# Cross-attention on one core: x in slices and Wo through ScalarE's queue, later weight loads, earlier residuals

## The chip, the cores and the metric

The kernel runs on one core of one Trainium2 chip, in float32. The metric is device microseconds of one execution. "us" is left out where a number is plainly a time.

The engines are named as the profile names them: PE (TensorE, matmuls; PEld is its weight load), DVE (VectorE), ACT (ScalarE), POOL (GpSimd) and SP (SyncE, which here only issues DMAs). A "q" behind an engine's name (ACTq, SPq) stands for that engine's instruction queue, where DMAs are issued and semaphores are waited for.

## The reference

x is (2, 2048, 640); the context is (2, 154, 1024), of which the first 77 rows are text and the other 77 an image prompt. There are 20 heads of 32.

```python
q = split_heads(x @ Wq.T)
k, v = split_heads(text @ Wk.T), split_heads(text @ Wv.T)
k_ip, v_ip = split_heads(ip @ Wk_ip.T), split_heads(ip @ Wv_ip.T)
out_text = softmax(q @ k.T / sqrt(32)) @ v
out_ip = softmax(q @ k_ip.T / sqrt(32)) @ v_ip
result = merge_heads(out_text + out_ip) @ Wo.T + bo + x
```

## The kernel before

**Tiles and steps.** Everything is kept transposed, with channels on partitions. The 4096 tokens (both batches) are cut into NBLK = 4 blocks of 1024 tokens, and the 640 channels into NC = 5 chunks of 128, which are four heads each. One step m = 5 j + c handles chunk c of block j; there are 20 steps, and one more round to finish the last. Blocks 0 and 1 are batch 0, blocks 2 and 3 batch 1.

**What one step does.** Scores of step m (L210) are computed in three groups of token tiles (3, 3 and 2) into the eight PSUM banks, LOW and HIGH four each. ScalarE copies them out (L222), VectorE takes maxima (L229), GpSimd subtracts them (L230), ScalarE takes the exponential (L236), VectorE sums (L243) and inverts (L245), GpSimd multiplies (L250), VectorE transposes 32 by 32 blocks (L261). In the same step TensorE also attends for step m - 1 (L273), whose result ScalarE copies to aT (L285), and it fills its time with other matmuls: `queries` for coming steps (L181, copied to qT by L189), and in steps 0 to 4 the keys and values of the next chunks (`project_kv`, L139, copied by L146 and L149), in later steps the output projection of finished blocks (`Out.step`, L308). An output piece of 128 channels by 512 tokens is finished on VectorE (`Out.store`, L319) with the bias and a residual piece of x that `Out.fetch` loads (L303), and is stored (L322).

**What sets the order.** The schedule is written out by hand: each engine runs its instructions in the order in which the code issues them, within the main loop over m. `plan(m)` names the filler work of a step in two lists, `after1` (behind the first two groups of scores) and `after2` (behind attention). `ahead` is how many of `after1` come before the first group's exponential (`soften(m, 0)`); the rest comes after it.

**DMAs before the change.** All but five loads of Wq at the start are issued from SyncE. They are, in the order of the code:

- `load_w` (L130): one 128-column piece of Wk, Wk_ip, Wv or Wv_ip, 512 KB, into one of five slots in the second aT buffer. It is called after every `project_kv`, which has freed a slot.
- `spread_v(c, b)` (L161): 16 small DMAs of 20 KB that copy the transposed V of chunk c (`vS`, written by `square_v`, L152) to four partition groups. Batch 0's are issued in steps 0 to 4, batch 1's in steps 6 to 10.
- `load_x` (L168): the next block of x as two loads of 1,280 KB, in the steps with c = 1.
- Wo (L495): one load of 1,600 KB at the end of step 4, into the space that held the context.
- the residuals, fetched up to FETCH = 3 pieces ahead of the stores, beginning in step 5, and the stores.

Of the kernel before, what the change touches and what calls it, by code (L numbers as in the profile page):

```python
# [19 lines left out]
def kernel(  # L20
# [25 lines left out]
    nc = tc.nc  # L46
    P = 128
    NC = C // P
    NCC = CC // P
    G = P // D  # L50
    TB = 512
    NH = 2
    BLK = NH * TB
    NT = BLK // P
    NBLK = B * S // BLK
# [6 lines left out]
    NM = NBLK * NC  # L62
# [4 lines left out]
    FETCH = 3  # L67
# [12 lines left out]
    def turn_to(half, n=G):  # L80


        turn[:] = half[:1] if n == 1 else (half[: min(n, G) - 1] + half[-1:]) * 2

    def bank():
        return turn.pop(0)
# [5 lines left out]
    xs = [const.tile([P, NC, BLK], F32, name=f"x_{n}") for n in range(2)]  # L92
# [14 lines left out]
    wo = wo_ct.rearrange("p (k o) -> p k o", k=NC)  # L107
# [6 lines left out]
    def block_of(m):  # L114

        j, c = divmod(m, NC)
        return j, c, j * BLK // S
# [7 lines left out]
    def load_w():  # L125
        n = len(loaded)
        if n < len(wlist):
            src, c = wlist[n]
            w = wslots[n % len(wslots)]
            nc.sync.dma_start(  # L130
                out=w, in_=src[:, ts(c, P)].rearrange("(k p) o -> p k o", p=P)
            )
            loaded.append(w)

    def project_kv(n, t):

        out = bank()[:, : B * L].rearrange("p (b l) -> p b l", b=B)
        for k in range(NCC):
            nc.tensor.matmul(  # L139
                out, loaded[n][:, k, :], cT[:, k, :, t, :], start=(k == 0), stop=(k == NCC - 1)  # L140
            )
        load_w()
        return out

    def project_k(c, t):
        nc.scalar.copy(kT[:, c, :, t, :], project_kv(4 * c + t, t))  # L146

    def project_v(c, t):
        nc.scalar.copy(vTs[c % 2][:, :, ds(t * L, L)], project_kv(4 * c + 2 + t, t))  # L149
# [7 lines left out]
    def spread_v(c, b):  # L157

        for g in range(G):
            for r in range(G):  # L160
                nc.sync.dma_start(  # L161
                    out=v4[r * D : (r + 1) * D, c, g].rearrange("p k d -> p (k d)"),
                    in_=vS[g * D : (g + 1) * D, c, b],
                )


    def load_x(j, h):
        nc.sync.dma_start(  # L168
            out=xs[j % 2][:, :, ts(h, TB)],
            in_=xT[:, ds(j * BLK + h * TB, TB)].rearrange("(c p) s -> p c s", p=P),  # L170
        )

    qTs = {}

# [28 lines left out]
    def scores(m, s, ps):  # L203

        _, c, b = block_of(m)
        first, n = GROUPS[s]
        for t in range(n):
            h, st = divmod(first + t, TB // P)
            for g in range(G):
                nc.tensor.matmul(  # L210
                    ps[g][:, ts(t, 2 * L)],
                    qTs[(m, h)][g * D : (g + 1) * D, ts(st, P)],
                    kT[g * D : (g + 1) * D, c, b].rearrange("p t l -> p (t l)"),
                    start=True,
                    stop=True,
                )

    def take(m, s, ps):

        n = GROUPS[s][1]  # L220
        for g in range(G):
            nc.scalar.copy(  # L222
                keys_of(m, s)[:, :, g], ps[g][:, : n * 2 * L].rearrange("p (n l) -> p n l", n=n)
            )
# [9 lines left out]
    def exponential(m, s):  # L234
        e = keys_of(m, s).rearrange("p n g l -> p (n g) l")
        nc.scalar.activation(e, e, AF.Exp, scale=SCALE)  # L236
# [3 lines left out]
    def sums(m, s):  # L240
        n = GROUPS[s][1] * G
        den = small.tile([P, n, 2], F32, tag=f"den{n}", name=f"den_{m}_{s}")
        nc.vector.tensor_reduce(den, rows_of(m, s), AX.X, ALU.add)  # L243
        rden = small.tile([P, n, 2], F32, tag=f"rden{n}", name=f"rden_{m}_{s}")
        nc.vector.reciprocal(rden, den)  # L245
        rdens[s] = rden

    def normalise(m, s):
        n = GROUPS[s][1] * G
        nc.gpsimd.tensor_tensor(  # L250
            rows_of(m, s), rows_of(m, s), rdens[s].unsqueeze(3).to_broadcast([P, n, 2, L]), ALU.mult
        )

    def soften(m, s):
        exponential(m, s)
        sums(m, s)
        normalise(m, s)

    def transpose(m, s):
        first, n = GROUPS[s]  # L260
        nc.vector.transpose(  # L261
            tT[:, first : first + n].rearrange("p n g k s -> p (n g k s)"),
            pb_of(m, s).rearrange("p n g l -> p (n g l)"),
        )
# [59 lines left out]
    outs = [Out(v) for v in range(NV)]  # L324
# [23 lines left out]
    def flush():  # L348
        for o in finished[len(stored) :]:
            o.store()  # L350
            stored.append(o)
            for o in outs[len(stored) : len(stored) + FETCH]:
                o.fetch()
# [15 lines left out]
    for k in (0, half):  # L369
        nc.sync.dma_start(  # L370
            out=wo_ct[:, ds(k * B * LT, half * B * LT)].rearrange("p (k n) -> p k n", k=half),
            in_=ctxT[ds(k * P, half * P), :].rearrange("(k p) n -> p k n", p=P),
# [17 lines left out]
    for t in range(2):  # L390
        project_k(0, t)

    def plan(m):

        q = [lambda h=h: queries(m + LEAD[h], h) for h in range(NH)]
        out = lambda: fill(NC)
        if m < NC:
            v = [lambda t=t: project_v(m, t) for t in range(2)]
            k = [lambda t=t: project_k(m + 1, t) for t in range(2) if m + 1 < NC]
            return q[:1] + v, k + q[1:]  # L400
        if m == NM - 1:
            return [out], [out] + [lambda: fill(NC - 1)] * OPEN
        if m == NM - 2:
            return [out], [out, q[1]]
        if m % NC == 0:
            return q, [out] * 2
        return [out, q[0]], [out, q[1]]

    def is_late(m):


        return m == NC or (m > NC and m % NC == 1)

    for m in range(NM + 1):
        j, c, _ = block_of(m)
        new = m < NM
        old = m >= 1
        after1, after2 = plan(m) if new else ([], [])
        flush()
        if new:  # L420
            for g, half in ((0, LOW), (1, HIGH)):
                scores(m, g, half)
            for g, half in ((0, LOW), (1, HIGH)):
                take(m, g, half)
        turn_to(LOW, len(after1))


        ahead = len(after1)
        if ahead > 1 and 2 < m < NM - 2 and c > 0:
            ahead -= 1  # L430
        short = new and (len(after1) == 1 or m == 0)
        late = is_late(m)
        if old and not late:
            transpose(m - 1, 2)
        if new:
            maxima(m, 0)
        if late:
            transpose(m - 1, 1)
        if new and not short:
            maxima(m, 1)  # L440
        if late:
            transpose(m - 1, 2)
        if c == 1 and j + 1 < NBLK:
            for h in range(NH):
                load_x(j + 1, h)
        for work in after1[:ahead]:
            work()
        flush()
        if new:
            if short:  # L450
                maxima(m, 1)
            else:
                soften(m, 0)
        for work in after1[ahead:]:
            work()
        flush()
        if m < NC:
            square_v(m)
            spread_v(m, 0)
        if new:  # L460
            scores(m, 2, HIGH)
        if old:
            attend(m - 1, LOW)
        if new:
            take(m, 2, HIGH)
            maxima(m, 2)
            if short:
                soften(m, 0)
                if old:
                    take_attention(m - 1, LOW)  # L470
            soften(m, 1)
            if short:
                soften(m, 2)
        if old:
            if not short:
                take_attention(m - 1, LOW)
            attended[(m - 1) // NC] += 1
            if (m - 1) // NC == NBLK // B - 1:
                spread_v((m - 1) % NC, 1)
        turn_to(HIGH, len(after2))  # L480
        if new:
            transpose(m, 0)
        for work in after2[:-1]:
            work()
        flush()
        if new and not short:
            soften(m, 2)
        for work in after2[-1:]:
            work()
        if m >= NC and (c == 0 or m == NM - 2):  # L490
            flush()
        if new and not is_late(m + 1):
            transpose(m, 1)
        if m == NC - 1:
            nc.sync.dma_start(out=wo, in_=WoT.rearrange("(c p) o -> p c o", p=P))  # L495
    turn_to(LOW)
    while len(finished) < NV:
        fill(NC)
# [33 lines left out]
```

## Time and profile before

Three executions took 538.38, 538.55 and 1334.83; the median is 538.55.

| | us |
|---|---|
| profiled execution | 538.22 |
| its span, first to last instruction | 536.4 |
| ScalarE waiting for queries (L189 <- PE L181), total | 99.5 |
| SyncE waiting to store (L322 <- DVE L319), total | 247.8 |
| one residual, 256 KB, issue to landing, median | 3.3 |
| one `load_x`, 1,280 KB, issue to landing, median | 8.7 |
| one spread, 20 KB, issue to landing, median | 1.8 |
| Wo, 1,600 KB, issue to landing | 7.0 |

The mean granted TensorE clock is 0.993. The DMA traffic is uneven: the page's 40 slices go from 9 to 308 GB/s, with a mean of 94. A time such as 61.75 below is counted from the start of the span. Step 1 begins with its scores at 45.08, step 2 at 74.48, step 3 at 97.73, step 4 at 121.55 and step 5 at 140.59. A matmul record counts passes: one score matmul of L210 makes two records, so "x24" are the 12 matmuls of one group of three tiles.

### The profile page before, as it was taken

The numbers are of one execution on the slowest core, as the hardware profiler recorded it, in microseconds if no ns is written. First come the engines' busy times: TensorE is split into PE (matmuls) and PEld (weight loads), VectorE is DVE, ScalarE is ACT, GpSimd is POOL, SyncE is SP. The second block draws the span as 40 slices with busy tenths as digits, with TensorE's granted clock in tenths as the row PEclk, the third lists the DMA queues.
The fourth block names the chain that finished last, engine by engine and source line by source line (L and its number), as shares of the span: only waits on it lengthen the run. The fifth ranks groups of instructions, "written<-read, shape, count | busy, mean of one in ns | idle before, by whom it ended". The sixth has DMA issues, their size and how long they took to land.

```text
span 536.4 us, 12754 instructions
## 1 busy us (share of the span) xinstructions
PE 522.8 (97%) x5614; PEld 289.0 (54%) x5614; DVE 378.1 (70%) x286; ACT 245.1 (46%) x441; POOL 351.0 (65%) x130
## 2 busy tenths in 40 slices
PE   8999799999999999999999999999999999999997
PEld 4676668677554545545454554544455454554442
DVE  0059765877878879787768978787678878888121
ACT  1255445456654444644454464445356464562000
POOL 0057947796967868668677866869576876978000
PEclk9999799999999999999999999999999999999999
DMA  8974733320136420221206311111112111131151
GB/s 258 308 208 138 243 94 88 97 59 9 32 138 221 150 89 25 82 65 48 57 16 221 144 41 40 42 39 42 38 41 75 45 42 40 40 101 40 61 187 67
DMA packets 50488, 50.60 MB, mean 94 GB/s; under 512 B 5248, under 2 KB 34432, under 8 KB 50432
## 3 DMA queue, kind: packets, MB, share of 16 engines
q1 hardware_dynamic: 49712, 49.45, 30.3%
q8 instruction: 44, 0.72, 0.6%
q10 hardware_dynamic: 720, 0.33, 0.2%
q14 instruction: 12, 0.10, 0.1%
HBM read 36.00 MB, written 10.49 MB: 87 GB/s over the span
## 4 chain that ended last, share of the span: by engine, by line
PE 87%; DVE 4%; issue 2%; DMA 2%; POOL 2%; ACT 1%; SPq 0%; ACTq 0%; DVEq 0%; POOLq 0%
PE bank L181 30%; PE bank L308 30%; PE bank L273 11%; PE bank L210 8%; PE bank L139 8%; DVE den L243 2%; POOL pb L250 2%; DVE mx L229 1%; DMA x<-in_x_dram 1%; ACT pb L236 1%; DVE ot L319 1%; DMA wq<-in_L_xattn_Wq_dram 1%; DMA res<-in_x_dram 1%; POOL pb L230 0%; DVE tT L261 0%
## 5 line engine op out<-in xcount | busy, mean ns | idle before, releaser
L230 POOL TENSOR_TENSOR pb<-pb,mx 128x1848 f32<-128x1848 f32 (+1 forms) x60 | 175.8, 2942 | 105.9 <-DVE mx L229 105.9
L250 POOL TENSOR_TENSOR pb<-pb,rden 128x1848 f32<-128x1848 f32 (+1 forms) x60 | 176.0, 2942 | 36.9 <-DVE rden L245 27.7
L181 PE MATMUL bank<-x,wq 128*128 128x512 f32 x400 | 180.0, 599 | 0.9 <-DMA x<-in_x_dram 0.9
L308 PE MATMUL bank<-aT,wo_ct 128*128 128x512 f32 x400 | 179.1, 599 | 0.9 <-ACT aT L285 0.9
L243 DVE TENSOR_REDUCE den<-pb 128x24 f32<-128x1848 f32 (+1 forms) x60 | 111.3, 1856 | 62.3 <-ACT pb L236 62.2
L229 DVE TENSOR_REDUCE mx<-pb 128x24 f32<-128x1848 f32 (+1 forms) x60 | 109.6, 1848 | 43.3 <-ACT pb L222 42.3
L236 ACT ACTIVATE pb<-pb 128x1848 f32<-128x1848 f32 (+1 forms) x60 | 95.1, 1587 | 87.4 <-POOL pb L230 87.4
L181 PEld LDWEIGHTS bank<-x,wq 128*128 128x128 f32 x400 | 75.4, 191 | 92.8 <-issue 87.4
L308 PEld LDWEIGHTS bank<-aT,wo_ct 128*128 128x128 f32 x400 | 73.7, 190 | 91.8 <-issue 83.8
L261 DVE STREAM_TRANSPOSE tT<-pb 128x1920 f32<-128x1920 f32 (+1 forms) x60 | 115.9, 1931 | 5.3 <-POOL pb L250 5.2
L222 ACT COPY pb<-bank 128x462 f32<-128x462 f32 (+1 forms) x240 | 101.1, 533 | 22.5 <-PE bank L210 21.2
L273 PE MATMUL bank<-tT,v 32*32 32x256 f32 x3200 | 70.5, 386 | 4.1 <-issue 3.6
L189 ACT COPY qT<-bank 128x512 f32<-128x512 f32 x40 | 23.4, 585 | 99.5 <-PE bank L181 99.5
L210 PEld LDWEIGHTS bank<-kT,qT 32*128 32x128 f32 x1280 | 44.7, 184 | 30.2 <-issue 19.6
L273 PEld LDWEIGHTS bank<-tT,v 32*32 32x32 f32 x3200 | 46.9, 103 | 21.9 <-issue 8.7
L210 PE MATMUL bank<-kT,qT 32*128 32x154 f32 x1280 | 54.8, 303 | 2.5 <-DVE ot L319 1.9
L319 DVE SCALAR_TENSOR_TENSOR ot<-bank,bo_sb,res 128x512 f32<-128x512 f32 x40 | 29.5, 739 | 37.6 <-PE bank L308 31.9
L139 PEld LDWEIGHTS bank<-wo_ct,aT 128*128 128x128 f32 x320 | 45.5, 197 | 5.2 <-issue 3.3
L139 PE MATMUL bank<-wo_ct,aT 128*128 128x154 f32 x320 | 46.9, 305 | 0.5 <-ACT pb L222 0.5
L285 ACT COPY aT<-bank 128x256 f32<-128x256 f32 x80 | 24.4, 391 | 17.2 <-PE bank L273 17.2
L245 DVE RECIPROCAL rden<-den 128x24 f32<-128x24 f32 (+1 forms) x60 | 17.2, 286 | 2.1
L146 ACT COPY kT<-bank 128x154 f32<-128x154 f32 x10 | 2.8, 286 | 15.1 <-PE bank L139 15.1
(12 smaller groups left out, 14.0 us busy)
## 6 DMA issues: line engine op xcount, KB each, us to landing
res<-in_x_dram SPq DMA_DIRECT2D x40, 256.0 KB, 3.3
out_dram<-ot SPq DMA_DIRECT2D x40, 256.0 KB, 2.4
x<-in_x_dram SPq DMA_DIRECT2D x6, 1280.0 KB, 8.7
v<-vS SPq DMA_DIRECT2D x160, 20.0 KB, 1.8
x<-in_x_dram SPq DMA_DIRECT2D x10, 256.0 KB, 5.0
aT<-in_L_xattn_Wk_dram SPq DMA_DIRECT2D x5, 512.0 KB, 7.0
aT<-in_L_xattn_Wk_ip_dram SPq DMA_DIRECT2D x5, 512.0 KB, 4.4
aT<-in_L_xattn_Wv_dram SPq DMA_DIRECT2D x5, 512.0 KB, 5.5
```

The costliest lines, as they stand in the source:

```text
L139: nc.tensor.matmul(out, loaded[n][:, k, :], cT[:, k, :, t, :], start=(k == 0), stop=(k == NCC - 1))
L181: nc.tensor.matmul(pq, wq[:, k, ts(c, P)], xs[j % 2][:, k, ts(h, TB)], start=(k == 0), stop=(k == NC - 1),)
L210: nc.tensor.matmul(ps[g][:, ts(t, 2 * L)], qTs[(m, h)][g * D : (g + 1) * D, ts(st, P)], kT[g * D : (g + 1) * D, c, b].rearrange("p t l -> ...
L222: nc.scalar.copy(keys_of(m, s)[:, :, g], ps[g][:, : n * 2 * L].rearrange("p (n l) -> p n l", n=n))
L229: nc.vector.tensor_reduce(mx, rows_of(m, s), AX.X, ALU.max)
L230: nc.gpsimd.tensor_tensor(rows_of(m, s), rows_of(m, s), mx.unsqueeze(3).to_broadcast([P, n, 2, L]), ALU.subtract)
L236: nc.scalar.activation(e, e, AF.Exp, scale=SCALE)
L243: nc.vector.tensor_reduce(den, rows_of(m, s), AX.X, ALU.add)
L250: nc.gpsimd.tensor_tensor(rows_of(m, s), rows_of(m, s), rdens[s].unsqueeze(3).to_broadcast([P, n, 2, L]), ALU.mult)
L261: nc.vector.transpose(tT[:, first : first + n].rearrange("p n g k s -> p (n g k s)"), pb_of(m, s).rearrange("p n g l -> p (n g l)"),)
L273: nc.tensor.matmul(pa[r][g * D : (g + 1) * D, : NT * D], v4[rows, c, g, k, :], tT[rows, :, g, k, :], start=(k == 0), stop=(k == NK - 1),)
L308: nc.tensor.matmul(self.po, wo[:, self.k, ts(self.o, P)], aTs[self.j % 2][:, self.k, ts(self.h, TB)], start=(self.k == 0), stop=(self.k == ...
```

## The change

- x of the next block is cut into ten slices of 256 KB (one chunk of channels, 512 tokens). They are put on a list in step 1 and then in the steps with c = 0 from step 5 on, and up to four of them are issued in a step, from ScalarE's queue, behind the last exponential of the step.
- Wo is issued from ScalarE's queue, in step 4, right behind the copies of the attention result. The first three residuals are asked for there too, on SyncE.
- `load_w` is called after a projection of K as before, but for V it is called inside `spread_v`, after the first four and after the first eight of the 16 small DMAs.
- The condition `c > 0` on `ahead` goes, so that in the steps 5, 10 and 15 the second of the two query projections is issued behind the first exponential.

No engine's arithmetic changes; the order of instructions on PE, DVE and POOL stays as it was. On ScalarE 31 DMAs come in between and one copy changes its place in three steps; on SyncE the DMAs are moved as said.

```diff
@@ project_kv / project_k
-        load_w()
         return out
     def project_k(c, t):
         nc.scalar.copy(kT[:, c, :, t, :], project_kv(4 * c + t, t))
+        load_w()
@@ spread_v
                     in_=vS[g * D : (g + 1) * D, c, b],
                 )
+            if b == 0 and g < 2:
+                load_w()
-    def load_x(j, h):
-        nc.sync.dma_start(
-            out=xs[j % 2][:, :, ts(h, TB)],
-            in_=xT[:, ds(j * BLK + h * TB, TB)].rearrange("(c p) s -> p c s", p=P),
-        )
+    slices = []
+    def load_x():
+        if slices:
+            j, h, k = slices.pop(0)
+            nc.scalar.dma_start(
+                out=xs[j % 2][:, k, ts(h, TB)], in_=xT[ts(k, P), ds(j * BLK + h * TB, TB)]
+            )
@@ main loop, before the work of after1
         ahead = len(after1)
-        if ahead > 1 and 2 < m < NM - 2 and c > 0:
+        if ahead > 1 and 2 < m < NM - 2:
             ahead -= 1
...
-        if c == 1 and j + 1 < NBLK:
-            for h in range(NH):
-                load_x(j + 1, h)
+        if m == 1 or (m >= NC and c == 0 and j + 1 < NBLK):
+            slices.extend((j + 1, h, k) for h in range(NH) for k in range(NC))
@@ main loop, behind the attention of m - 1
             if not short:
                 take_attention(m - 1, LOW)
             attended[(m - 1) // NC] += 1
+            if m == NC - 1:
+                nc.scalar.dma_start(out=wo, in_=WoT.rearrange("(c p) o -> p c o", p=P))
+                for o in outs[:FETCH]:
+                    o.fetch()
@@ main loop, end of a step
         if new and not short:
             soften(m, 2)
+        for _ in range(4):
+            load_x()
         for work in after2[-1:]:
             work()
...
-        if m == NC - 1:
-            nc.sync.dma_start(out=wo, in_=WoT.rearrange("(c p) o -> p c o", p=P))
```

## The prediction

> **What bounds the kernel now.** Times are in us. I read the page's busy shares first, then who waited for whom.
>
> ```profile
> PE 522.8 (97%) x5614; PEld 289.0 (54%) x5614; DVE 378.1 (70%) x286; ACT 245.1 (46%) x441; POOL 351.0 (65%) x130
> ...
> PEclk9999799999999999999999999999999999999999
> ```
>
> TensorE is the bound: it idles only 536.4 - 522.8 = 13.6 of the span, so hardly more than that can be won, while any wait put before it adds in full. Only the fifth of the 40 slices (53.6 to 67) has a lower clock. The list of waits (engine and line, what it waited for, total, times, longest) says where the idle time is; the second answer is of SyncE's queue:
>
> ```profile
> PE bank L273 <- issue: 3.6, 3, 2.7
> ...
> PE bank L210 <- DVE ot L319: 1.9, 2, 1.3
> ```
>
> ```profile
> SPq L366 <- DMA wq<-in_L_xattn_Wq_dram: 2.0, 1, 2.0
> ```
>
> The first two are this change's targets. The third is SyncE's queue at the start: a load of x held back for a load of Wq on another engine's queue, with which it shares no data. The built program says why: all DMAs use eight completion semaphores in turn, and each waits, at its issuer, for the DMA that had the same one before. I come back to that. Next the 1-us windows round the first stall (busy PE, PEld, DVE, ACT, POOL; then granted clock, DMA share, GB/s):
>
> ```profile
> 61.00:62.00 1.00, 0.00 (x0) 0.00 (x0) 0.97 (x4) 1.00 (x1) 0.50 (x1) 0.81 1.22 301
> 62.00:63.00 1.00, 0.77 (x19) 0.24 (x19) 1.00 (x2) 0.41 (x2) 1.00 (x1) 0.50 0.54 130
> ...
> 68.00:69.00 1.00, 1.00 (x8) 1.00 (x7) 0.00 (x0) 0.08 (x1) 1.00 (x1) 0.78 0.12 28
> ```
>
> TensorE stands from 59.5 to 62.2 waiting for no engine, and starts as the DMA traffic drains: I read it as its own instructions stuck behind x (two 1,280 KB loads issued at 48.05) and the weights of 53.56 and 55.67. The clock then stays at 0.50 until 68. The chain of waits prices that: the 32 matmuls of L139 take 6.91 there and 4.41 at 89.09 (2.5), the last 19 of L273 1.12 against about 0.4 (160 take 3.39): 3.2 lost to the clock. This stall costs 2.7 + 3.2 = 5.9.
>
> **Part 1: x away from SyncE, weights later (m = 1).** With 2,560 KB of x and 1,024 KB of weights gone from 48 to 59, I count the 5.9 as won. What is late next? In program order ScalarE's queue gets four x slices at the end of m = 1, after the last exponential and before the copy of qT. By the built program they wait for the landing of the 11th to 14th of the 16 spreads of V; SyncE issues those one by one:
>
> ```profile
> 61.75 10.55 SPq L161 DMA_DIRECT2D v<-vS  x16
> ...
> 74.59 0.58 ACT L189 COPY qT<-bank 128x512 f32<-128x512 f32 x1 [2.87 <-PE bank L181]
> ```
>
> One spread takes 10.55 / 16 = 0.66. They start after VectorE's transpose of V at 61.27, which hangs on the softmax chain and not on the stall, so still at 61.75. Two weight loads now lie among the first eight (0.6 each with the gap). The 14th starts at 61.75 + 13 x 0.66 + 1.2 = 71.5, lands 1.8 later (the spreads' median; 73.3), the slice takes 0.45 to issue (Wq slices on ScalarE: median 453 ns), the copy 0.58: 74.4. That ScalarE's engine stands while its queue issues is seen at the start: five issues from 0.73 take 2.34, its table load begins at 3.10. TensorE without the stall runs 59.65 (end of attention) + 4.4 (keys) + 4.3 (queries) + 0.9 (the first 24 score matmuls) = 69.3, then needs the bank that this copy empties: it stands 5.1. That is longer than the 2.7 which cost the clock before, so the clock falls again: +3.2. Net -5.9 + 5.1 + 3.2 = +2.4. Bounds: -0.8 if the clock holds; +3.9 if a spread lands 3.3 after its issue (the slowest at m = 2), being queued behind 512 KB of weights.
>
> **m = 2**, the same with no stall to win back:
>
> ```profile
> 89.85 10.77 SPq L161 DMA_DIRECT2D v<-vS  x16
> ...
> 97.73 1.85 PE L210 MATMUL bank<-kT,qT 32*128 32x154 f32 x48
> 97.83 0.58 ACT L189 COPY qT<-bank 128x512 f32<-128x512 f32 x1 [1.47 <-PE bank L181]
> ```
>
> 14th spread at 89.85 + 13 x 0.67 + 1.2 = 99.8, landed 101.6, slice issued 102.1, copy done 102.6; TensorE needs it at 97.73 + 0.9 = 98.7. Stall 4.0 to 5.5 by the same landing bounds; I take 4.3, since most land at 1.8. With the clock 7.5 (4.0 to 8.7). At m = 3 two slices wait for the 9th and 10th spread: 112.05 + 9 x 0.68 + 0.6 + 1.8 = 120.6, before the copy at 121.66: nothing.
>
> **Part 2: Wo on ScalarE's queue (m = 4).** It is queued right after the attention copies and waits for the 12th spread; behind it are the last exponential and the qT copy:
>
> ```profile
> 134.82 10.82 SPq L161 DMA_DIRECT2D v<-vS  x16
> ...
> 141.23 0.56 ACT L189 COPY qT<-bank 128x512 f32<-128x512 f32 x1
> ...
> 141.85 1.07 PE L210 MATMUL bank<-kT,qT 32*128 32x154 f32 x24 [0.20 <-ACT qT L189]
> ```
>
> ScalarE reaches it at 137.0 (copies of L285: 135.80 + 1.20). The 12th spread starts at 134.82 + 11 x 0.68 = 142.3, lands 144.1; issue 0.53 (as on SyncE), exponential 1.24 (now at 140.09), copy 0.57: 146.4 in place of 141.8. TensorE waits for exactly this copy already (0.20), so all of 4.6 shows, and with the clock 7.8 (4.6 to 9.3). SyncE saves that one issue, which nobody waited for.
>
> **Part 3: residuals early; one more query behind the softmax.** The second store of m = 5 waits 1.2 for its residual and TensorE 1.3 for that store (166.27, 167.08). Asked for at m = 4, the residual has landed: -1.3; VectorE is next at 165.1, when TensorE has just come. Without "c > 0" the exponentials at m = 5, 10, 15 go ahead of a query copy, which at m = 10 frees them from 271.0 back to about 268.4; the stores come earlier, and the other 0.6 of the wait on L319 goes. Nobody waits for the copy put behind. Together -1.9 (0 to -2.5).
>
> **Part 4: the other slices.** Issuing 4 x 0.45 = 1.8 per step lies in ScalarE's idle time before the copy of qT (3.92 to 4.91 at m = 6 and 7); uncovered it would cost up to 1.8. The fourth slice of m = 6 and of m = 10 waits for the first's landing, 3.4 (residuals of equal size) to 5.0 (x at the start): at m = 6 ScalarE is free at 188.8 to 190.4, wanted at 189.8; at m = 10 at 283 to 287, wanted at 284.4. I take +0.6 in all (0 to 4). SyncE's later DMAs wait for slices in turn; the residuals lie three outputs ahead: nothing.
>
> **Sum.** 2.4 + 7.5 + 7.8 - 1.9 + 0.6 = +16.4. The profiled execution took 538.22 (span 536.4), 0.3 under the median of the runs: 538.55 + 16.4 = 555.
>
> **Two rules beside these rows.** The Trainium skill ("TensorE: Matmul & The Clock Gate", Part 1) has the clock fall after an idle window of about 3.4 us and return after a busy one; here 2.7 sufficed, and the half clock lasted 6 after work resumed. By the page each fall would cost some 1.7, an estimate, and the sum be near 550. "DMA: Bandwidth & Descriptors" (Issuing engines are not separate DMA queues) says that DMAs from SyncE and ScalarE share the same 16 engines and that a second issuer saves only issue time; by it the move itself is worth nothing, which speaks against this change; the 5.9 would come from timing alone.
>
> **The rivals.** (a) *The clock does not fall* in the three new stalls: 555 - 3 x 3.2 = 545. For it: the wait of 1.3 at 167 left it at 1.00. Against: 2.7 did not, and these are 4 to 5. (b) *The stalls do not come* and the kernel is faster: ScalarE passes its DMAs because the spreads have landed, or runs on past them. Price: -5.9 - 1.9 = -7.8, 531. It decides if the 14th spread of m = 2 lands by 98, that is if the spreads take 0.4 and not 0.67 each. For it: ScalarE is busy only 46%. Against: SyncE's spread rows are alike at m = 1, 2 and 4. (c) *The change does not do what it says*: the fetch stall stays, as weights alone hold it up. Then the wait of m = 1 lies under it: 555 - 2.4 = 553.
>
> **Chances.** Forecast 0.62 (its own range 548 to 563), (a) 0.15, (b) 0.15, (c) 0.06, anything else 0.02. From 541 to 563 holds the forecast, (a) and (c) with their bounds, and leaves out (b). Beyond 2% (10.8, about what a measurement can tell from no change): slower than 549.3 are the forecast and (c), 0.65; (a), (b) and the forecast's lower end are within, 0.32; below 527.8 lies only what goes beyond (b), 0.03.
>
> **What would show it.** Fetch step: no "issue" wait of 2.7 for L273 near 59.5, clock 1.00 from 60 to 68. Stalls: ScalarE's queue waiting on DMA v at the lines of x and Wo, 4 to 7 at m = 1, 2, 4; TensorE's L210 waiting some 4 to 5 each for the qT copy; three dips to 0.50. Residuals: no wait of L319 for a DMA at 166. Wrong if ScalarE's DMA lines show no wait.

## The result, and the profile after

The changed kernel takes 555.0, the median of six runs (552.9 to 556.68), against 537.85 before, the median of six runs in all (536.99 to 538.55, and the one of 1334.83). The ratio is 1.0316, with a 95% interval from 1.0286 to 1.0345: slower, and the predicted time is met. The one execution of 1334.83 lies far above all others and is not in the ratio. The profiled execution took 555.08; its span is 553.3, which is 16.9 more than before, at a mean granted clock of 0.981.

The page's busy shares and its row of the clock, after the change:

```profile
PE 527.3 (95%) x5614; PEld 290.1 (52%) x5614; DVE 378.9 (68%) x286; ACT 245.8 (44%) x441; POOL 351.0 (63%) x130
...
PEclk9999979799979999999999999999999999999999
```

TensorE runs the same 5614 matmul records, so no work was added, but it idles 553.3 - 527.3 = 26.0 in place of 13.6, and is busy 4.5 longer for the same records. One dip of the clock (slice 5, counted from 1) has become three (slices 6, 8 and 12). The list of TensorE's waits:

```profile
PE bank L216 <- ACT qT L195: 15.2, 3, 5.4
PE bank L279 <- issue: 2.5, 3, 1.3
...
PE bank L187 <- DMA x<-in_x_dram: 0.8, 1, 0.8
```

The first line is new: the score matmuls (L210 before, L216 now) stand three times for the copy of qT on ScalarE. The attention's wait without a releaser has its longest at 1.3, no longer at 2.7, and the wait on the output store (L210 on L319 before, now L216 on L325) is gone from the list. The last line is no news: it lies at 9.8 to 10.6, where the kernel starts, and such a wait of 0.9 was there before. What held ScalarE up is in the same list for ScalarE:

```profile
ACT qT L195 <- DMA x<-in_x_dram: 10.1, 2, 6.9
ACT pb L242 <- DMA v<-vS: 7.8, 1, 7.8
ACT qT L195 <- issue: 6.2, 1, 6.2
```

ScalarE stands at a copy whose data are long there, and at an exponential, "for" x slices that nothing in that copy reads, and for a spread of V. The timeline of the changed kernel at steps 1, 2 and 4 (start, duration, engine or queue, line; in brackets the idle time before it and its releaser) shows the order:

```profile
61.50 2.41 SPq L161 DMA_DIRECT2D v<-vS  x4
...
66.78 1.23 ACT L242 ACTIVATE pb<-pb 128x1232 f32<-128x1232 f32 x1 [2.50 <-POOL pb L236]
...
67.75 5.02 SPq L161 DMA_DIRECT2D v<-vS  x8
68.17 1.32 PE L216 MATMUL bank<-kT,qT 32*128 32x154 f32 x30
72.18 2.01 ACTq L175 DMA_DIRECT2D x<-in_x_dram  x4
...
74.23 0.59 ACT L195 COPY qT<-bank 128x512 f32<-128x512 f32 x1 [6.22 <-issue]
...
74.87 1.90 PE L216 MATMUL bank<-kT,qT 32*128 32x154 f32 x18 [5.37 <-ACT qT L195]
...
103.08 2.50 ACTq L175 DMA_DIRECT2D x<-in_x_dram  x4
...
106.26 1.90 PE L216 MATMUL bank<-kT,qT 32*128 32x154 f32 x18 [4.89 <-ACT qT L195]
...
144.51 10.82 SPq L161 DMA_DIRECT2D v<-vS  x16
145.49 1.20 ACT L291 COPY aT<-bank 128x256 f32<-128x256 f32 x4
...
154.07 0.39 ACTq L483 DMA_DIRECT2D wo_ct<-in_L_xattn_Wo_dram  x1
154.50 1.23 ACT L242 ACTIVATE pb<-pb 128x1232 f32<-128x1232 f32 x1 [7.81 <-DMA v<-vS]
155.64 0.57 ACT L195 COPY qT<-bank 128x512 f32<-128x512 f32 x1
156.26 1.93 PE L216 MATMUL bank<-kT,qT 32*128 32x154 f32 x24 [4.92 <-ACT qT L195]
```

At step 1 ScalarE ends its exponential at 68.01 and issues the first slice at 72.18, in the middle of SyncE's spreads (61.50 to 72.77); only then comes the copy of qT, and TensorE, which had its other scores done at 69.49, goes on at 74.87. At step 4 ScalarE is free at 146.69 and Wo is issued at 154.07; the exponential and the copy behind it are late, and TensorE with them.

The trace also names the completion semaphore of each DMA and the time at which it was last raised, and this ties each wait to its spread. At step 1 the four slices use the semaphores of the 11th to the 14th spread; the 11th has landed at 72.16, and the first slice leaves at 72.18. At step 2 the 14th spread has landed at 105.22, and the fourth slice leaves at 105.25. At step 4 Wo uses the semaphore of the 12th spread, which has landed at 153.99, and leaves at 154.07.

The clock of the changed kernel in 1-us windows (busy PE, PEld, DVE, ACT, POOL; granted clock, DMA share, GB/s):

```profile
59.00:60.00 1.00, 1.00 (x29) 0.59 (x17) 1.00 (x1) 0.91 (x3) 1.00 (x1) 1.00 0.06 16
...
75.00:76.00 1.00, 1.00 (x16) 1.00 (x17) 0.00 (x0) 1.00 (x3) 0.00 (x0) 0.50 0.91 283
80.00:81.00 1.00, 1.00 (x3) 0.48 (x2) 0.70 (x1) 0.00 (x0) 1.00 (x1) 0.73 0.26 71
...
111.00:112.00 1.00, 1.00 (x4) 0.44 (x3) 1.00 (x1) 0.00 (x0) 1.00 (x1) 0.87 0.93 262
...
162.00:163.00 1.00, 1.00 (x3) 0.28 (x3) 1.00 (x2) 0.00 (x0) 1.00 (x1) 0.77 0.33 115
```

The first row is where the old stall began: now TensorE is busy at full clock, with hardly any DMA traffic. After each of the three waits the clock is at 0.50; the last rows say when it returns. A mean of 0.73 over one us is 0.54 of it at half speed, so the clock is back at about 80.5, and likewise at 111.3 and 162.5. From TensorE's restarts at 74.87, 106.26 and 156.26 that is 5.7, 5.0 and 6.2 of work at half clock.

### The profile page after: what moved, and what is told of

The parts are those of the page before. It is cut to its first block, busy times and chain, and to the rows that moved or that the text cites. A ratio compares the mean times of both kernels' runs of the same rounds, so it can differ in the third digit from the quotient of the medians.

```text
span 553.3 us, 12770 instructions
## 1 busy us (share of the span) xinstructions
PE 527.3 (95%) x5614; PEld 290.1 (52%) x5614; DVE 378.9 (68%) x286; ACT 245.8 (44%) x441; POOL 351.0 (63%) x130
## 4 chain that ended last, share of the span: by engine, by line
PE 80%; DMA 5%; SPq 4%; DVE 3%; ACT 3%; issue 2%; POOL 1%; ACTq 0%; POOLq 0%
PE bank L314 32%; PE bank L187 26%; PE bank L279 10%; PE bank L216 8%; PE bank L139 4%; SPq L161 4%; ACT pb L242 2%; DVE den L249 2%; DMA aT<-in_L_xattn_Wk_ip_dram 1%; DMA x<-in_x_dram 1%; DMA v<-vS 1%; POOL pb L256 1%; DMA wq<-in_L_xattn_Wq_dram 1%; POOL pb L236 1%; SPq L376 1%
## 5 line engine op out<-in xcount | busy, mean ns | idle before, releaser
L187 PE MATMUL bank<-x,wq 128*128 128x512 f32 x400 | 184.7, 611 | 1.2 <-DMA x<-in_x_dram 0.8
L249 DVE TENSOR_REDUCE den<-pb 128x24 f32<-128x1848 f32 (+1 forms) x60 | 111.3, 1855 | 62.8 <-ACT pb L242 62.8
L187 PEld LDWEIGHTS bank<-x,wq 128*128 128x128 f32 x400 | 77.1, 196 | 96.7 <-issue 88.7
L216 PE MATMUL bank<-kT,qT 32*128 32x154 f32 x1280 | 57.4, 312 | 15.6 <-ACT qT L195 15.2
L216 PEld LDWEIGHTS bank<-kT,qT 32*128 32x128 f32 x1280 | 47.0, 191 | 43.1 <-issue 16.4
L325 DVE SCALAR_TENSOR_TENSOR ot<-bank,bo_sb,res 128x512 f32<-128x512 f32 x40 | 29.6, 743 | 45.3 <-PE bank L314 36.7
L139 PEld LDWEIGHTS bank<-wo_ct,aT 128*128 128x128 f32 x320 | 43.1, 188 | 5.2 <-issue 3.3
L139 PE MATMUL bank<-wo_ct,aT 128*128 128x154 f32 x320 | 44.4, 294 | 0.7 <-ACT pb L228 0.5
L149 ACT COPY vT<-bank 128x154 f32<-128x154 f32 x10 | 2.9, 290 | 13.4 <-PE bank L139 13.4
```

Of the source, the lines that this page charges most:

```text
L139: nc.tensor.matmul(out, loaded[n][:, k, :], cT[:, k, :, t, :], start=(k == 0), stop=(k == NCC - 1))
L187: nc.tensor.matmul(pq, wq[:, k, ts(c, P)], xs[j % 2][:, k, ts(h, TB)], start=(k == 0), stop=(k == NC - 1),)
L216: nc.tensor.matmul(ps[g][:, ts(t, 2 * L)], qTs[(m, h)][g * D : (g + 1) * D, ts(st, P)], kT[g * D : (g + 1) * D, c, b].rearrange("p t l -> ...
```

## The experiments

The theory: each DMA on ScalarE's queue waits there for the DMA that used the same completion semaphore before, a spread of V; ScalarE's later work waits with it, then TensorE, and each of these waits drops the clock. Rivals: the later weights or the slices themselves are to blame wherever they are issued from; or the clock does not matter. Ratios are to the kernel before, run on the same chip, with a 95% interval.

### 1. The same DMAs from SyncE

```diff
-            nc.scalar.dma_start(
+            nc.sync.dma_start(
                 out=xs[j % 2][:, k, ts(h, TB)], ...
-                nc.scalar.dma_start(out=wo, in_=WoT.rearrange("(c p) o -> p c o", p=P))
+                nc.sync.dma_start(out=wo, in_=WoT.rearrange("(c p) o -> p c o", p=P))
```

> The change with its x slices and Wo issued from SyncE's queue, at the same places in the code; all else as changed. Theory (ScalarE stands at its DMAs until spreads of V have landed, TensorE waits for the copy behind them, and the clock falls after each of the three waits): the waits of 5.4, 4.9 and 4.9 us and the three dips to 0.50 go, and the fetch stall at 59.5 stays away: 555 - 15.2 - about 8.5 = 531. Rival (the smaller pieces, the later weights or the DMA traffic slow TensorE, whoever issues): still above 545.

Measured: 539.11, ratio 1.004 (1.0021 to 1.0059). ScalarE's waits are gone, and 16 of the time with them, but not 24. The list of TensorE's waits of this run has a line that no theory had:

```profile
PE bank L187 <- DMA x<-in_x_dram: 7.1, 2, 6.2
```

Its timeline at step 2 says which DMA that is:

```profile
97.10 2.43 SPq L175 DMA_DIRECT2D x<-in_x_dram  x4
...
103.28 2.08 PE L187 MATMUL bank<-x,wq 128*128 128x512 f32 x2 [6.22 <-DMA x<-in_x_dram]
```

The queries of block 1 need all five chunks of the first 512 tokens. Four slices go out per step, so the fifth is asked for only at the end of step 2, here at 97.10, and TensorE stands for it from 97.06. (The other 0.9 of the 7.1 lies at the start, as before.) In the change the same slice is asked for at 103.08 and no wait for it shows, since TensorE was already late through ScalarE. One dip of the clock stays. Experiment 2 tests this reading.

### 2. The same with five slices in a step

```diff
-        for _ in range(4):
+        for _ in range(5):
             load_x()
```

(on top of experiment 1)

> All DMAs on SyncE as in the first experiment, with five slices a step in place of four, so that the first half block (five slices) is asked for in step 1. Theory (in the first experiment the waits at ScalarE's queue were gone, and the 6.2 us of TensorE waiting for x and its dip of the clock, about 2.5, came from the fifth slice, asked for only in step 2): that wait goes, 539.1 - 8.5 = 530.5. Rival (x on SyncE is late because SyncE is late as a whole): still above 536, with TensorE waiting for x.

Measured: 531.73, ratio 0.9866 (0.9818 to 0.9914). The wait for x is gone, and the page has one full row of clock:

```profile
PE 518.7 (98%) x5614; PEld 285.7 (54%) x5614; DVE 378.8 (71%) x286; ACT 245.9 (46%) x441; POOL 350.9 (66%) x130
...
PEclk9999999999999999999999999999999999999999
```

All parts of the change together are worth 538.4 - 531.7 = 6.7 once no slice and no Wo is on ScalarE's queue and the fifth slice is early.

### 3. The same DMAs on ScalarE, ahead of the spreads

The theory blames what is in flight when the DMA is issued, not the engine. So the 31 DMAs stay on ScalarE, and are issued just before the spreads instead of behind or among them.

```diff
+        for _ in range(4):
+            load_x()
+        if m == NC - 1:
+            nc.scalar.dma_start(out=wo, in_=WoT.rearrange("(c p) o -> p c o", p=P))
...
             spread_v(m, 0)
...
-                nc.scalar.dma_start(out=wo, in_=WoT.rearrange("(c p) o -> p c o", p=P))
...
-        for _ in range(4):
-            load_x()
```

> The change with the slices and Wo still on ScalarE's queue, but issued in the same steps just before the spread of V instead of behind it, so that their completion semaphores were last used by DMAs of the step before. Theory (what costs is the wait for the step's own spreads): the three waits go; four issues of 0.45 us now lie before the copies of the third group, which may cost TensorE 1 to 2 us at step 1: 531 to 534. Rival (issuing from ScalarE is itself what costs): 545 or more.

Measured: 530.79, ratio 0.9883 (0.9854 to 0.9912), 24 below the change with the same DMAs on the same engine. The timeline of this run at step 1:

```profile
56.76 2.11 ACTq L175 DMA_DIRECT2D x<-in_x_dram  x4
...
61.34 3.15 SPq L161 DMA_DIRECT2D v<-vS  x4
...
68.28 1.85 PE L216 MATMUL bank<-kT,qT 32*128 32x154 f32 x48
...
68.39 0.58 ACT L195 COPY qT<-bank 128x512 f32<-128x512 f32 x1 [0.54 <-PE bank L187]
```

The slices leave before the first spread, the copy of qT waits for nothing but its own matmuls, and the scores run in one piece of 48. TensorE idles 529.2 - 518.8 = 10.4 at a mean clock of 1.000. With experiment 2 this is the fastest version measured; both beat the kernel before, by 1.2 and 1.3%.

### 4. Wo alone back on SyncE, at the end of step 4

```diff
-                nc.scalar.dma_start(out=wo, in_=WoT.rearrange("(c p) o -> p c o", p=P))
...
+        if m == NC - 1:
+            nc.sync.dma_start(out=wo, in_=WoT.rearrange("(c p) o -> p c o", p=P))
```

> The change with Wo alone put back to SyncE's queue at the end of step 4. Theory: the wait of 4.9 us at the start of step 5 and its dip of the clock (about 3) go, the two of steps 2 and 3 stay: 555 - 8 = 547. Rival (Wo's transfer itself, which then runs in step 5, costs the time): 553 or more.

Measured: 548.04, ratio 1.0213 (1.0174 to 1.0251): 7.0 less than the change, where the prediction had put 7.8 to Wo. In the list of TensorE's waits one of three is gone, and a small new one came, of the output projection for Wo, which is now asked for behind the spreads and the residuals:

```profile
PE bank L216 <- ACT qT L195: 9.8, 3, 4.9
...
PE bank L314 <- DMA wo_ct<-in_L_xattn_Wo_dram: 1.6, 1, 1.6
```

Of the three waits that the first line counts the third is 0.20, as at that place before. Without the new 1.6 the removal is worth 8.6.

### 5. Work for TensorE in the three waits

Extra matmuls of 128 by 512, whose results are overwritten, were put where TensorE stands, to hold the clock up while ScalarE stays as late as before. First 10, 9 and 9 of them:

```diff
+                if g == 1 and m in (2, 3, NC):
+                    for _ in range(10 if m == 2 else 9):
+                        nc.tensor.matmul(HIGH[2], wq[:, 0, :P], wq[:, 0, :TB], start=True, stop=True)
```

> The change with 10, 9 and 9 extra matmuls of 128x512 into an unused bank (results overwritten) where TensorE stands in steps 2, 3 and 5; ScalarE's waits are left as they are. Theory (the clock falls because TensorE is idle for some 5 us, and that is a loss beside the wait): waits for the qT copy end at the same times, the clock stays at 1.00, 555 - 8.5 = 546.5. Rival (the waits are all of the loss, or the clock falls by the DMA traffic): 553 to 555, with the dips still there.

Measured: 553.23, ratio 1.0296 (1.0264 to 1.0328), with the clock at 1.00 throughout. The time says nothing on its cost, since I had sized the work by half: each such matmul in float32 makes two records of 0.44, and the extra work lasted 8.85, 7.99 and 7.99, which is 3.5, 3.1 and 3.1 more than the waits it covers. So five each:

> The run before this with 5 extra matmuls at each of the three places in place of 10, 9 and 9: those lasted 8.9, 8.0 and 8.0 us and so were longer than the waits of 4.9 to 5.4, since one such matmul makes two passes of 0.44 us. Five last 4.4 and end before the copy. Theory (idle time drops the clock, and that is a loss beside the wait): remaining waits about 1 us or less, clock 1.00 throughout, 555 - 8.5 = 546.5. Rival (the half clock falls in time in which TensorE would have waited anyway for the softmax, or comes from the DMA traffic): 552 to 555.

Measured: 545.48, ratio 1.0121 (1.0077 to 1.0165). TensorE's waits and the page's clock in this run:

```profile
PE bank L216 <- ACT qT L195: 1.6, 3, 0.9
```

```profile
PEclk9999999999999999999999999999999999999999
```

The extra work fits into the waits: 1.6 of 15.2 is left, and ScalarE is as late as before. TensorE's useful work starts as late as in the change, but at full clock, and 555.0 - 545.5 = 9.5 is gone (10.5 by the difference of the two ratios, 0.0195 of 537.85). Most of that is the clock's share, but not all: TensorE's waits without a releaser also fell, from 2.5 in the change to 0.7 in this run. What is left, 7.7 to 8.7, agrees with the 8.4 read from the windows (half of 5.7 + 5.0 + 6.2), which is 2.5 to 3.1 for each wait. So the clock does matter, and with the same DMA traffic it stays up when TensorE has work: it falls by the idle time.

### 6. The weights alone

In the kernel before, only `load_w` for V moves into `spread_v`.

```diff
-        load_w()
         return out
     def project_k(c, t):
         nc.scalar.copy(kT[:, c, :, t, :], project_kv(4 * c + t, t))
+        load_w()
...
+            if b == 0 and g < 2:
+                load_w()
```

> The kernel before with only the weights behind V moved into the spread; x still in two large loads in step 1. Theory (TensorE's instruction fetch near 59.5 stands behind whatever bytes are queued): 1,024 KB less are 2.7 us at 380 GB/s, so the traffic ends near 58.9, and the stall of 2.7 and its dip of the clock go nearly or wholly: 531 to 534. Rival (the large loads of x hold the fetch up by themselves): stall stays, 536 to 538.

Measured: 536.68, ratio 0.9985 (0.9953 to 1.0017): no difference. The stall stays, as the timeline of this run shows:

```profile
49.01 2.20 SPq L170 DMA_DIRECT2D x<-in_x_dram  x2
...
61.28 1.02 PE L275 MATMUL bank<-tT,v 32*32 32x256 f32 x19 [2.44 <-issue]
```

No weights are asked for between 49 and 63, and still TensorE stands 2.44: x alone does it. (In this run the wait on the output store was 1.64 in place of 1.29, and the clock fell a second time, from about 167.3 to 170.7; so the time alone, without the timeline, would not decide.)

### 7. The x slices alone

In the kernel before, only x is cut up and moved to ScalarE, at the places of the change (its hunks on `slices`, `load_x` and the end of a step).

> The kernel before with only the x slices moved to ScalarE's queue; weights and Wo as before. Theory: the fetch stall at 59.5 goes (2,560 KB less); at steps 2 and 3 ScalarE waits for the 11th to 14th spread, without the two loads in between 1.2 us less than in the change: waits of about 3.9 and 3.0, the clock falling at the first or at both; no wait at step 5: 543 to 546. Rival (weights alone hold the fetch up): a stall near 59.5 stays, and the wait of step 2 lies under it.

Measured: 551.62, ratio 1.023 (1.0185 to 1.0274), some 6 more than expected. The stall near 59.5 shrank to 0.72, and the two waits for qT are there (4.39 and 3.75). The rest is a third wait. The timeline of this run at step 5:

```profile
172.41 1.79 ACTq L173 DMA_DIRECT2D x<-in_x_dram  x4
...
173.44 1.52 SPq L307 DMA_DIRECT2D res<-in_x_dram  x3
...
178.98 0.75 DVE L323 SCALAR_TENSOR_TENSOR ot<-bank,bo_sb,res 128x512 f32<-128x512 f32 x1 [3.58 <-DMA res<-in_x_dram]
...
179.78 1.85 PE L214 MATMUL bank<-kT,qT 32*128 32x154 f32 x18 [3.69 <-DVE ot L323]
```

The residuals are asked for 1.0 behind four slices of x, the store waits 3.58 for one and TensorE 3.69 for the store; the clock drops a third time. In the change the first three residuals are asked for in step 4, and no such wait shows. That the early residuals are what keeps the slices of step 5 from costing a wait is likely but not shown: the change also takes out the condition on c, which moves the stores, and no run parts the two here.

### 8. The residuals and the condition on c

In the kernel before, first both, then the condition alone:

```diff
-        if ahead > 1 and 2 < m < NM - 2 and c > 0:
+        if ahead > 1 and 2 < m < NM - 2:
...
+            if m == NC - 1:
+                for o in outs[:FETCH]:
+                    o.fetch()
```

> The kernel before with only the first three residuals asked for in step 4 and without the condition c > 0. Theory: TensorE's waits of 1.9 on the stores of L319 (1.3 of it for a residual in step 5) go, the fetch stall at 59.5 stays: 1.9 us less than before, ratio 0.9965. Rival (the residual was hidden, or the time is given back later): ratio 1.000.

> The kernel before with only the condition c > 0 taken out. Theory: the wait for the residual in step 5 (1.3) stays, since it was asked for late; of the other 0.6 at steps 10 and 15 most goes: 0.5 less than before, ratio 0.999. Rival (the query copy put behind the exponential is late, and attention waits for its bank): up to 1 us a step in three steps, ratio 1.002 to 1.006, with TensorE waiting for the qT copy.

Measured: both 536.09, ratio 0.9989 (0.9968 to 1.001), which is not told from no change; the condition alone 533.96, ratio 0.9943 (0.9924 to 0.9962), more than expected. (Part of that is the clock, see below.) TensorE's waits, first of the run with both, then of the condition alone:

```profile
PE bank L308 <- DMA wo_ct<-in_L_xattn_Wo_dram: 1.2, 1, 1.2
...
PE bank L210 <- DVE ot L319: 0.7, 1, 0.7
```

```profile
PE bank L210 <- DVE ot L319: 0.7, 1, 0.7
```

The wait for the store falls from 1.9 to 0.7 in both, so taking out the condition is enough to remove the 1.2; the early residuals by themselves were not run. Without the condition the first store of step 5 comes at 159.01 rather than 161.98 (1.3 of this had been gained before step 5), the next residual is asked for as much earlier, and the store that waited is past before TensorE needs its bank. The early residuals add nothing to this here, and being ahead of Wo on SyncE's queue they cost a wait of 1.2 for Wo. Not all of the 3.1 is the condition's. TensorE's idle time in that profile is 533.4 - 519.8 = 13.6, as before, and 3.0 of busy time is gone, of which work at half clock for 3.4 in place of 6.2 explains 1.4. That half clock lies at 62 to 65, and the condition acts first in step 5, near 140, so this part is how the clock happened to fall. It is so over all runs: the mean granted clock was 0.9974 in the nine runs of the condition alone, 0.9953 in the twelve with both and 0.9953 in the twenty of the kernel before, and 0.0021 of 537 is 1.1. Where the rest comes from is not settled.

## Why the prediction was right, step by step

| term of the sum | predicted | measured in the profile after |
|---|---|---|
| fetch stall at 59.5, idle | -2.7 | -2.7 |
| its clock | -3.2 | -3.2: clock 1.00 there now |
| wait of step 1 | +5.1 | +5.37 |
| wait of step 2 | +4.3 | +4.89 |
| wait of step 4 | +4.6 | +4.92 |
| clock of the three | +9.6 | +8.4: half of 5.7 + 5.0 + 6.2 |
| wait for the stores | -1.9 | -1.9 |
| other slices | +0.6 | 0 |
| shorter fetch waits at 432, 476 and 497 | none | +1.6: 2.5, where 0.9 was left of 3.6 |
| sum | +16.4 | +17.4, of a span 16.9 longer |

The 0.5 that the terms exceed the span by are not placed. The sum came closer than its terms, which is luck: the three waits were 1.2 longer than predicted and their clock cost 1.2 less.

**Part 1.** The step "I count the 5.9 as won" was right, and experiments 6 and 7 sharpen it: removing the weights from that stretch did nothing (2.44 stays), removing x did it (0.72 left). The step from the 14th spread to the copy of qT was right, expected done at 74.4 and done at 74.82, but two errors offset each other in it: the 14th spread landed at 72.70 and not at 73.3, and the fourth slice was issued at 74.19, 1.5 after that and not 0.45. Experiment 3 shows the mechanism by place, the semaphores show it DMA by DMA. At step 2 the prediction's own times give a wait of 4.0 (102.6 - 98.6), and it took 4.3. The spreads began 2.3 later than before, and the copy was done 1.3 later than the estimate shifted by that: the 14th spread started 0.7 later and took 2.4 to land in place of 1.8. So 4.89, inside the bounds of 4.0 to 5.5.

**The clock.** "The clock falls again" held three times out of three; experiment 5 prices it in time at some 8 (9.5 less shorter waits of 1.8 that are not the clock's), against 9.6 predicted and 8.4 read from the windows. Rival (a) fell with it; that its 545 is so near the 545.48 which experiment 5 measured with the clock held up is in part those 1.8. The Trainium skill ("TensorE: Matmul & The Clock Gate", Part 1) would let waits of 4.9 to 5.4 drop the clock, as they did; it would not let 2.71, 2.44 and 1.64 do so, which they did (before, and experiment 6). Its return after a busy window agrees with all 14 falls in the twelve traces: the clock came back at the end of the first interval of 3.41 that was work throughout (the last section has the times). For this change the rows were the better price.

**Part 2.** Right: 4.92 against 4.6, and 7.0 in time in experiment 4 (8.6 without the new wait for Wo) against 7.8.

**Part 3.** The sum was right and its split was not borne out. "-1.3" was put to the early residuals and 0.6 to the condition; experiment 8 shows 1.2 for the condition and nothing more for the residuals on top of it. What the two do in the change may be another thing, which the prediction did not see: without the early residuals and with the condition in place, the slices of step 5 cost a wait of 3.69 and a dip (experiment 7).

**Part 4.** "+0.6" was 0: at step 6 the copy of qT stood 3.2 behind the slices, and TensorE did not wait for it; at step 10 nothing was late. The prediction missed that the fifth slice is asked for only in step 2. This cost nothing here, because ScalarE's waits lay over it, and 6.2 and a dip in experiment 1, once they were gone.

**Rivals (b) and (c).** (b) needed spreads of 0.4; the eight of step 1 took 5.02 / 8 = 0.63. Its 531 is what the change is worth when the stalls are really absent: 531.73 and 530.79. (c) was wrong: with the weights left in place and only x moved (experiment 7), 0.72 of the 2.71 stayed. The rule of "DMA: Bandwidth & Descriptors" (Issuing engines are not separate DMA queues), by which a second issuer gains no transfer rate, agrees with experiments 2 and 3: 531.73 from SyncE, 530.79 from ScalarE. The 24 that the second issuer lost here came of its place in the order and not of the transfers.

## What to carry to other kernels

A DMA put on a compute engine's queue brings its own waits into that engine's order: look up which earlier DMA used its completion semaphore, and issue it ahead of a burst of small DMAs. Price a new TensorE wait of some 2 us or more with the clock as well as with its length: here three waits of 15.2 in all cost some 8 more through it. When a late transfer is moved, look for the next one that was hidden under it, and try the parts of a change alone, since one may be there to cover another.

## What the runs showed of the hardware

- TensorE can stand for its own instructions while bulk loads are in flight: 2.71 before, 2.44 without the weights, 0.72 with x in slices elsewhere. The page of the kernel before lists the packets that carry instructions (queue 8):

```profile
q8 instruction: 44, 0.72, 0.6%
```

They are 16 KB each, and the traces have their times. The third moves from 59.49 to 60.64 in the kernel before, among x and the weights, and from 56.48 to 57.62 in the changed kernel, though the attention began at 56.30 and 56.05. So it came some 2.8 late, and TensorE went on 1.6 after it. In the twelve traces there are 27 waits of the attention over 0.4 without a releaser, and each ends 1.2 to 1.6 after such a packet. That queue 8 serves TensorE is read from this agreement.

- The half clock came in spells of two lengths only. Leaving out start and end, the granted clock of the twelve traces has 14 of them: nine of 6.82 or 6.83 and five of 3.41 or 3.42. The nine began while TensorE still stood, 0.6 to 1.9 before it went on. The five began when it was at work again, up to 1.8 after it went on. Within one execution the falls lie whole multiples of 3.413 apart: 30.72 and 51.20 (9 and 15 times) in the changed kernel, 105.81 (31 times) in experiment 6. So the clock is set at fixed intervals of 3.41, whose place in the kernel differs from run to run, and it came back at the end of the first that was work throughout.
- An idle time of 1.64 within one such interval dropped the clock to 0.50 (experiment 6), 1.8 after work had resumed; one of 1.29 in the kernel before did not.
- The half clock covered 3.4 of work in the short spells and 5.0 to 6.2 in those of the kernel before and the change, so one fall cost 1.7 to 3.1. The length of the wait does not set it: 2.71 led to 6.2 and 3.1 to 3.4.
- A float32 matmul of 128 by 512 shows as two records of 0.44.
